# A list-scheduled attention and gated-graph kernel: the planner's figures for transfers, and the ranks of its last three batches

## The chip, the cores and the metric

The kernel runs on one core of a Trainium2 chip. Its time is the device time of one execution in microseconds, and of several executions the median is given. A core has a matmul engine (PE, with its weight loads as PEld), a vector engine (DVE), an activation engine (ACT), a general engine (POOL), and a queue engine (SP) that here only issues transfers. Each works through its own list of instructions in the order in which they were written. An instruction that waits for another engine or a transfer holds up everything behind it on its own engine.

## The reference

Two layers over 16 batches of 1024 nodes with 128 features, with one adjacency matrix of 1024 x 1024 for all:

```python
# layer 0: attention over pairs, then a residual and a layernorm
h = x @ others_weight
e = leaky_relu((h @ a1)[:, idx1] + (h @ a2)[:, idx2])
att = softmax(where(adj > 0, e, NEG_BIG), axis=1)
x = layernorm(x + att @ h + x @ self_weight)
# layer 1: five gated steps over the same graph, then a residual and a layernorm
def step(h):
    m_in = m_out = adj @ h
    av = concatenate([m_in, m_out], -1)
    u3 = h @ u3_w.T + u3_b
    z = sigmoid(av @ w3_w.T + w3_b + u3)
    r = sigmoid(av @ w4_w.T + w4_b + u3)
    hv = tanh(av @ w5_w.T + w5_b + (r * h @ u5_w.T + u5_b))
    return (1 - z) * h + z * hv
y = x
for _ in range(5):
    y = step(y)
x = layernorm(x + y)
```

Batches don't depend on each other. Within a batch the five steps do, each on the one before.

## The kernel before

Everything of a batch is kept as 128 partitions by 1024 columns and worked on in two halves of 512. The state is held twice: turned with features on the partitions (`hT`, 32-bit), and with nodes on the partitions as a pair of a rounded part and its remainder (`hN`), so that a product with the adjacency matrix can be made from two faster passes.

One step of one batch, `step(b, s)`: for each half, 16 matmuls of `hN` with the adjacency matrix (L888), copied to `m` by ACT (L906). Then, per half, a product of `hT` with the weights `u3` (L919), which ACT copies into a second accumulator (L922), so that the gate products of `m` (L929) are added onto it there; two tanh on ACT (L932) for r and z; r times `hT` on DVE (L939); two products into `ps_g_v` (L945 of `m`, L946 of r); a tanh on ACT (L949); three DVE operations (L956, L963, L970) that write the new `hT`. After that the state has to be turned into `hN` for the next step. `flip` does this in most places: DVE transposes blocks of 32 x 32 into `T` (L488), SP issues four stores of 64 KB into a buffer `D` in device memory in a permuted order (L493) and then one load of 256 KB back into `F` (L497), which waits for the stores. ACT casts `F` to the first part of `hN` (L507) and DVE subtracts for the second (L511); this is `split`. In the first two batches' layer 0, and in the last step of the last three batches, PE transposes instead (`on_pe`).

`layer0(b)` makes the attention layer: loads of `xt` (L526), a row vector brought to all partitions through device memory (`ud`, `pb`, `uu`: L583, L590, L597), the products at L759, and a layernorm whose statistics are on DVE (L451, L453), whose power is four POOL operations (L457 to L460), and whose scaling is on ACT (L465). The output layernorm works in the same way and ends in two stores on SP (L1013). Sixteen further loads of the adjacency matrix (`look`, L1033) feed a check of the input by DVE.

The order of all this isn't that of the loops. Every operation is given to `Plan.add` with an engine, a length in ns, a rank, what it reads and what it writes. `Plan.order` then plays the program through: whenever an engine is free it takes, of the operations that are ready, the one of lowest rank that finds its buffers free, and an operation becomes ready when the last that it depends on has ended, plus a lag. The order in which operations start there is the order in which they are written into the queues. Lags are per engine: from SP to anything 2500 ns, from PE 250, DVE 150, ACT 170, POOL 200. Lengths of DVE and ACT are taken times 1.2. So four stores of a flip count as 280 ns of SP and 2500 of lag, the load back as 70 and 2500, the load of `xt` as 2700 and 2500, and POOL's part of a layernorm as 2200 of POOL.

Ranks come from `rank_of(b, s)`, with a small addition for each kind of operation (0.3 for r, 0.8 for `split`, 4 for the output store, minus 7 for the first loads of layer 0). A batch starts 5 ranks after the one before, and a step 3 ranks after the one before, but for the last two batches. Buffers limit how many batches can be under way: four each of `hN`, `hT` and `y0`, three of `T` and `F`, six of `D`, six accumulators `ps`.

Of the kernel before, what the change touches and what calls it, by code (L numbers as in the profile page):

```python
# [30 lines left out]
class Plan:  # L31
# [11 lines left out]
    def __init__(self, slots):  # L43
        self.slots = dict(slots)
        self.ops = []
        self.writer, self.readers = {}, {}

    def add(self, engine, length, rank, emit, reads=(), writes=()):
        i = len(self.ops)
        deps = {self.writer[v] for v in reads if v in self.writer}  # L50
        for v in writes:
            deps |= self.readers.pop(v, set())
            if v in self.writer:
                deps.add(self.writer[v])
        for v in reads:
            self.readers.setdefault(v, set()).add(i)
        for v in writes:
            self.writer[v] = i
        deps.discard(i)
        tiles = {v[0] for v in (*reads, *writes) if v[0][0] in self.slots}  # L60
        if engine in ("DVE", "ACT"):
            length *= self.MARGIN
        self.ops.append((engine, length, rank, emit, deps, tiles))

    def order(self):
        ops, free = self.ops, dict(self.slots)
        users, left = [[] for _ in ops], []
        uses = {}
        for i, (_, _, _, _, deps, tiles) in enumerate(ops):
            left.append(len(deps))  # L70
            for d in deps:
                users[d].append(i)
            for t in tiles:
                uses[t] = uses.get(t, 0) + 1
        ready, busy, live = {}, {}, set()
        at = {}
        events = [(0, 0, i) for i in range(len(ops)) if not left[i]]
        heapq.heapify(events)
        started = []
        while events:  # L80
            now = events[0][0]
            while events and events[0][0] == now:
                _, what, i = heapq.heappop(events)
                engine, _, rank, _, _, tiles = ops[i]
                if what == 0:
                    heapq.heappush(ready.setdefault(engine, []), (rank, i))
                elif what == 1:
                    busy.pop(engine)
                    for t in tiles:
                        uses[t] -= 1  # L90
                        if not uses[t]:
                            free[t[0]] += 1
            more = True
            while more:
                more = False
                for engine, queue in ready.items():
                    if engine in busy:
                        continue
                    later = []
                    while queue:  # L100
                        rank, i = heapq.heappop(queue)
                        _, length, _, _, _, tiles = ops[i]
                        new = [t for t in tiles if t not in live]
                        if all(free[t[0]] > 0 for t in new):
                            for t in new:
                                free[t[0]] -= 1
                                live.add(t)
                            started.append(i)
                            busy[engine] = more = True
                            heapq.heappush(events, (now + length, 1, i))  # L110
                            for u in users[i]:
                                left[u] -= 1
                                lag = self.SAME[engine] if ops[u][0] == engine else self.LAG[engine]
                                at[u] = max(at.get(u, 0), now + length + lag)
                                if not left[u]:
                                    heapq.heappush(events, (at[u], 0, u))
                            break
                        later.append((rank, i))
                    for x in later:
                        heapq.heappush(queue, x)  # L120
        assert len(started) == len(ops)
        return started
# [3 lines left out]
def kernel(  # L126
# [52 lines left out]
    nc = tc.nc  # L179
    B = x_t.shape[0]  # L180
# [26 lines left out]
    def exact(pools):  # L207
# [45 lines left out]
        def T(t, dtype=None, shape=None):  # L253
            if t not in tiles:
                _, sh, dt, _ = kinds[t[0]]
                tiles[t] = places[t[0]].tile(
                    shape or sh, dtype or dt, tag=t[0], name="_".join(map(str, t)).replace("-", "n")
                )
            return tiles[t]
# [25 lines left out]
        def sp(*a, **k):  # L285
            plan.add("SP", *a, **k)
# [8 lines left out]

        def rank_of(b, s):

            if b >= B - 2:
                return 5 * B - 10 + 3.25 * s if b == B - 2 else 5 * B - 7 + 2.75 * s
            return 5 * b + 3 * s  # L300


        boot = ("hl", "boot")
# [14 lines left out]
        def early_loads():  # L318
# [28 lines left out]
            writes=[(boot, "early"), (ws, "early"), (x0, "early"), (("xt", 1), "early"), *((t, "early") for t in staged)],  # L347
# [134 lines left out]
        def flip(name, src, read, dst, write, rank):  # L482


            t, d = ("T", *name), ("D", *name)

            def turn():
                nc.vector.transpose(T(t).rearrange("p (b c i) -> p b c i", b=4, c=4), turned(src()))  # L488

            def away():  # L490
                swapped = T(d).rearrange("(b i) (a x) -> a i b x", b=4, a=4)
                for k in range(4):
                    nc.sync.dma_start(swapped[k], T(t)[32 * k : 32 * (k + 1), :].rearrange("i (b x) -> i b x", b=4))  # L493

            dve(V, rank, turn, reads=read, writes=[(t, 0)])
            sp(280, rank, away, reads=[(t, 0)], writes=[(d, 0)])
            sp(70, rank, lambda: nc.sync.dma_start(dst(), T(d)), reads=[(d, 0)], writes=[write])  # L497

        def split(b, s, g, src, read, rank):

# [16 lines left out]
        def layer0(b):  # L517

            first = rank_of(b, 0) - (60 if b == 0 else 0)
            rank = first + D["l1"]  # L520
            xt, hx, pb, u, us, uu, ud = (
                ("xt", b), ("hx", b), ("pb", b), ("u3", b), ("us", b), ("uu", b), ("ud", b)
            )
            q, zs, rz, yT, y0, hT = ("q", b), ("zs", b), ("rz", b), ("yT", b), ("y0", b), ("hT", b)
            if b >= 2:
                sp(2700, rank, lambda: nc.sync.dma_start(T(xt), x_t[b]), writes=[(xt, 0), (xt, 1)])  # L526

            for g in range(4):
                ph = ("ps", "g", b, "ph", g)
# [37 lines left out]
            if b >= 2:  # L567
# [10 lines left out]
                    280, rank, lambda: nc.vector.tensor_copy(T(us), T(put)[0 : 3 * NC, 0:P]), reads=[(put, 0)], writes=[(us, 0)]  # L578
                )
                sp(  # L580
                    60,
                    rank,
                    lambda: nc.sync.dma_start(T(ud).rearrange("t (c p) -> (t c) p", p=P), T(us)),  # L583
                    reads=[(us, 0)],
                    writes=[(ud, 0)],
                )
                sp(
                    60,
                    rank,
                    lambda: nc.sync.dma_start(T(pb), T(ud)[2:3, :].to_broadcast([P, N])),  # L590
                    reads=[(ud, 0)],
                    writes=[(pb, 0), (pb, 1)],
                )

                def uu_():
                    for w in range(2):
                        nc.sync.dma_start(T(uu)[:, w, :], T(ud)[w].rearrange("(c p two) -> two p c", p=P, two=2)[w])  # L597

                sp(120, rank, uu_, reads=[(ud, 0)], writes=[(uu, 0)])

            else:

# [275 lines left out]
        def step(b, s):  # L878
# [96 lines left out]
            for g in range(2):  # L975
                gs = slice(4 * g, 4 * g + 4)
                o = ("o", b)

                def h(g=g):
                    return T(hT)[:, g * HALF : (g + 1) * HALF]  # L980

                if on_pe(b, s):
                    t = ("ps", "t", b, s, g)
                    transposes(h, [(hT, g)], t, rank + D["tr"])

                    def n(t=t):
                        return T(t).rearrange("p (c a j) -> p c a j", c=4, a=4)

                else:
                    t = ("F", b, s, g)  # L990
                    flip((b, s, g), h, [(hT, g)], lambda t=t: T(t), (t, 0), rank + D["tr"])

                    def n(t=t):
                        return chunks(T(t))

                if s < STEPS - 1:
                    split(b, s + 1, g, n, [(t, 0)], rank + D["split"])
                    continue

                def last(n=n, g=g, gs=gs):  # L1000
                    dst = T(o)[:, gs, :].rearrange("p c (a j) -> p c a j", a=4)
                    nc.vector.tensor_tensor(dst, n(), T(y0)[:, gs, :].rearrange("p c (a j) -> p c a j", a=4), ALU.add)

                dve(V, rank + D["o"], last, reads=[(t, 0), (y0, g)], writes=[(o, "raw", g)])
                
                def at(j, g=g):
                    return T(o)[:, 4 * g + j, :]

                layernorm(o, g, rank + D["ln"], (o, "raw", g), at, at, (o, g))
                sp(  # L1010
                    60,
                    rank + D["out"],
                    lambda gs=gs: nc.sync.dma_start(  # L1013
                        out[b].rearrange("(c p) d -> p c d", p=P)[:, gs, :], T(o)[:, gs, :]
                    ),
                    reads=[(o, g)],
                )
# [332 lines left out]
```

## Time and profile before

| | |
|---|---|
| median of 3 runs | 1540.07 us (1539.38 to 1541.79) |
| the profiled execution | 1543.68 us, of which the span from the first to the last instruction is 1541.8 |
| mean granted clock of PE | 0.989 |
| PE, DVE, ACT, POOL busy | 1501.8, 991.0, 813.3, 150.3 us |
| matmuls | 5204 |
| longest waits of SP | for T from DVE 521.2 us, for stores into D to land 120.9, for the scaled output from ACT 114.4 |
| waits of ACT at the cast of hN for F | 221.5 us in 96 waits, the longest 9.0 |

Durations come from the one profiled execution, which was 3.6 us above the median. A matmul's recorded duration overlaps the next one's, so busy shares of PE near 100% say that it never stood still, and the time between two starts says what one costs. A line of the waits view reads: the engine and line that waited, for whom, us in total, number of waits, longest. In a timeline a row merges like instructions that follow each other.

### The profile page before, as it was taken

What the parts mean: (1) busy time and instruction counts of PE and PEld (TensorE: products, weight loads), DVE (VectorE), ACT (ScalarE), POOL (GpSimd) and SP (SyncE); (2) the same over time, 40 slices, a digit from 0 to 9 for tenths busy, and PEclk for the clock granted to TensorE, in tenths of its full rate; (3) what the DMA queues carried; (4) which work ended last, traced back from release to release, by engine and by line L of the source; (5) the groups of instructions that cost most, each with busy time, mean ns of one, the idle gap of its engine ahead of it and who ended that gap; (6) DMA issues with size and microseconds to landing.
All of it is one profiled execution on the core that took longest, in us unless ns stands there. A gap on an engine that the chain in (4) does not pass through costs nothing.

```text
span 1541.8 us, 17536 instructions
## 1 busy us (share of the span) xinstructions
PE 1501.8 (97%) x5204; PEld 947.1 (61%) x5204; DVE 991.0 (64%) x2438; ACT 813.3 (53%) x1656; POOL 150.3 (10%) x266
## 2 busy tenths in 40 slices
PE   9889999999999999999999999999999999999996
PEld 7556665666656666666566656656666566666563
DVE  6555777757566675756757566675756777554644
ACT  5554544556454555545555454555636565544544
POOL 0001010011110201111011110201111012000101
PEclk9889999999999999999999999999999999999998
DMA  4013444333433324334243433324334233322121
GB/s 170 26 50 100 115 134 139 92 107 90 110 96 93 100 75 116 95 91 113 74 116 89 114 92 89 102 74 119 90 92 114 69 105 109 96 80 65 47 76 36
DMA packets 193981, 144.83 MB, mean 94 GB/s; under 512 B 33279, under 2 KB 158934, under 8 KB 193878
## 3 DMA queue, kind: packets, MB, share of 16 engines
q1 hardware_dynamic: 193314, 142.78, 33.2%
q8 instruction: 43, 0.70, 0.2%
q10 hardware_dynamic: 564, 0.85, 0.2%
q14 instruction: 60, 0.49, 0.1%
HBM read 79.95 MB, written 63.61 MB: 93 GB/s over the span
## 4 chain that ended last, share of the span: by engine, by line
PE 60%; DMA 15%; DVE 10%; SPq 5%; ACT 4%; issue 3%; POOL 2%; ACTq 0%; DVEq 0%; POOLq 0%
PE ps_acc L888 24%; PE ps_acc_po L759 6%; PE ps_g_v L946 6%; PE ps_g_r L919 6%; PE ps_g_r L929 6%; PE gz L929 5%; PE ps_g_v L945 5%; DMA F<-D 5%; SPq L493 4%; DMA D<-T 3%; DMA uu<-ud 2%; DMA F_y<-D_y 1%; DVE hv L956 1%; DVE T L488 1%; DVE hv L963 1%
## 5 line engine op out<-in xcount | busy, mean ns | idle before, releaser
L888 PE MATMUL ps_acc<-adj,hN 128*128 128x512 f32 x2560 | 686.4, 420 | 0.7 <-ACT y L465 0.7
L888 PEld LDWEIGHTS ps_acc<-adj,hN 128*128 128x128 f32 x2560 | 483.7, 189 | 176.4 <-issue 65.1
L511 DVE TENSOR_TENSOR hN<-F,hN 128x512 fp32r<-128x512 f32 x128 | 88.5, 691 | 191.2 <-ACT hN L507 191.0
L507 ACT CAST hN<-F 128x512 fp32r<-128x512 f32 x128 | 79.1, 618 | 221.7 <-DMA F<-D 221.5
L906 ACT COPY m<-ps_acc 128x512 f32<-128x512 f32 x160 | 93.1, 583 | 177.8 <-PE ps_acc L888 177.8
L946 PE MATMUL ps_g_v<-r,u5h 128*128 128x512 f32 x320 | 164.6, 596 | 12.9 <-DVE r L939 12.9
L956 DVE TENSOR_TENSOR hv<-hv,hT 128x512 f32<-128x512 f32 x160 | 109.3, 683 | 104.8 <-ACT hv L949 104.6
L929 PE MATMUL ps_g_r<-m,wm 128*128 128x512 f32 x320 | 163.8, 593 | 0.8 <-ACT gz L922 0.7
L945 PE MATMUL ps_g_v<-m,wm 128*128 128x512 f32 x320 | 163.4, 592 | 0.0
L929 PE MATMUL gz<-m,wm 128*128 128x512 f32 x320 | 163.4, 592 | 0.0
L949 ACT ACTIVATE hv<-ps_g_v,b 128x512 f32<-128x512 f32 x160 | 109.0, 685 | 86.7 <-PE ps_g_v L946 86.1
L919 PE MATMUL ps_g_r<-hT,u 128*128 128x512 f32 x320 | 153.9, 601 | 0.7 <-ACT hT L871 0.7
L939 DVE SCALAR_TENSOR_TENSOR r<-r,hT 128x512 f32<-128x512 f32 x160 | 109.6, 687 | 58.1 <-ACT r L932 57.6
L759 PE MATMUL ps_acc_po<-adj,hl 128*128 128x512 f32 x512 | 138.5, 421 | 0.3 <-DVE hl L742 0.3
L932 ACT ACTIVATE r<-ps_g_r,bh 128x512 f32<-128x512 f32 x160 | 109.9, 689 | 29.0 <-PE ps_g_r L929 28.6
L759 PEld LDWEIGHTS ps_acc_po<-adj,hl 128*128 128x128 f32 x512 | 96.1, 188 | 36.3 <-issue 14.4
L946 PEld LDWEIGHTS ps_g_v<-r,u5h 128*128 128x128 f32 x320 | 59.9, 190 | 93.3 <-issue 58.1
L932 ACT ACTIVATE z<-gz,bh 128x512 f32<-128x512 f32 x160 | 108.8, 686 | 6.8 <-PE gz L929 6.8
L970 DVE SCALAR_TENSOR_TENSOR hT<-hv,hT 128x512 f32<-128x512 f32 x160 | 108.4, 678 | 5.3
L963 DVE SCALAR_TENSOR_TENSOR hv<-z,hv 128x512 f32<-128x512 f32 x160 | 107.9, 675 | 2.1
L488 DVE STREAM_TRANSPOSE T<-hT 128x512 f32<-128x512 f32 x154 | 108.4, 705 | 1.2
L929 PEld LDWEIGHTS gz<-m,wm 128*128 128x128 f32 x320 | 60.8, 190 | 76.5 <-issue 76.5
(134 smaller groups left out, 1309.9 us busy)
## 6 DMA issues: line engine op xcount, KB each, us to landing
D<-T SPq DMA_DIRECT2D x616, 64.0 KB
F<-D SPq DMA_DIRECT2D x154, 256.0 KB
out_dram<-o SPq DMA_DIRECT2D x32, 256.0 KB
xt<-in_x_dram SPq DMA_DIRECT2D x15, 512.0 KB
pb<-ud SPq DMA_DIRECT2D x14, 512.0 KB
D_y<-T_y SPq DMA_DIRECT2D x112, 64.0 KB
F_y<-D_y SPq DMA_DIRECT2D x28, 256.0 KB
D_b<-T_b SPq DMA_DIRECT2D x112, 64.0 KB
```

The costliest lines, as they stand in the source:

```text
L488: nc.vector.transpose(T(t).rearrange("p (b c i) -> p b c i", b=4, c=4), turned(src()))
L759: nc.tensor.matmul(T(po), hl[:, k, c, :], adj[:, c, hs], start=(first and i == 0), stop=(last and i == len(terms) - 1),)
L888: nc.tensor.matmul(T(pm), T(hN)[:, k, c, :], adj[:, c, hs[e]], start=(c == 0 and k == 0), stop=(c == NC - 1 and k == 1),)
L919: nc.tensor.matmul(T(pr), u3, h(), start=True, stop=True)
L929: nc.tensor.matmul(T(p_), wm[:, j, :], T(m), start=False, stop=True, skip_group_check=True)
L932: nc.scalar.activation(T(t), T(p_), AF.Tanh, bias=bh[:, j : j + 1], scale=0.5)
L939: lambda r=r, h=h: nc.vector.scalar_tensor_tensor(T(r), T(r), 1.0, h(), ALU.add, ALU.mult),
L945: nc.tensor.matmul(T(pv), wm[:, 2, :], T(m), start=True, stop=False)
L946: nc.tensor.matmul(T(pv), u5h, T(r), start=False, stop=True)
L949: nc.scalar.activation(T(hv), T(pv), AF.Tanh, bias=b5, scale=1.0)
L956: lambda hv=hv, h=h: nc.vector.tensor_tensor(T(hv), T(hv), h(), ALU.subtract),
L963: lambda hv=hv, z=z: nc.vector.scalar_tensor_tensor(T(hv), T(z), 1.0, T(hv), ALU.add, ALU.mult),
```

## The change

Three edits, none of which adds or removes an instruction. The planner can be told a lag for a single operation. The SP operations get other lengths and, some of them, such a lag. And the ranks of the last three batches are drawn from a start and an end for each, where the last two had their own formula.

```diff
-    def add(self, engine, length, rank, emit, reads=(), writes=()):
+    def add(self, engine, length, rank, emit, reads=(), writes=(), lag=None):
         i = len(self.ops)
+        if lag is not None:
+            self.lag[i] = lag
...
                                 lag = self.SAME[engine] if ops[u][0] == engine else self.LAG[engine]
+                                lag = self.lag.get(i, lag)
...
         def rank_of(b, s):
-            if b >= B - 2:
-                return 5 * B - 10 + 3.25 * s if b == B - 2 else 5 * B - 7 + 2.75 * s
-            return 5 * b + 3 * s
+            if b < B - 3:
+                return 5 * b + 3 * s
+            begin = 5 * b - 2 * (b - B + 3)
+            end = 5 * B + 4 - 2 * (B - 1 - b)
+            return begin + (end - begin) * s / 4
...
-            sp(280, rank, away, reads=[(t, 0)], writes=[(d, 0)])
-            sp(70, rank, lambda: nc.sync.dma_start(dst(), T(d)), reads=[(d, 0)], writes=[write])
+            sp(1830, rank, away, reads=[(t, 0)], writes=[(d, 0)], lag=1500)
+            sp(450, rank, lambda: nc.sync.dma_start(dst(), T(d)), reads=[(d, 0)], writes=[write], lag=2300)
...
-                sp(2700, rank, lambda: nc.sync.dma_start(T(xt), x_t[b]), writes=[(xt, 0), (xt, 1)])
+                sp(450, rank, lambda: nc.sync.dma_start(T(xt), x_t[b]), writes=[(xt, 0), (xt, 1)], lag=3500)
```

The store of `ud` goes from 60 to 450 ns, the load of `pb` from 60 to 450 with a lag of 3000, the two loads of `uu` from 120 to 950 with a lag of 3000, and the output store from 60 to 450. The loads of `look` keep 60 ns and 2500.

With B = 16 the ranks of steps 0 to 4 are:

| batch | before | after |
|---|---|---|
| 13 | 65, 68, 71, 74, 77 | 65, 68.75, 72.5, 76.25, 80 |
| 14 | 70, 73.25, 76.5, 79.75, 83 | 68, 71.5, 75, 78.5, 82 |
| 15 | 73, 75.75, 78.5, 81.25, 84 | 71, 74.25, 77.5, 80.75, 84 |

More of the change, by code (lines that the diff above doesn't have):

```diff
@@ L45, in __init__ @@
         self.ops = []
+        self.lag = {}
         self.writer, self.readers = {}, {}
-    def add(self, engine, length, rank, emit, reads=(), writes=()):
+    def add(self, engine, length, rank, emit, reads=(), writes=(), lag=None):
         i = len(self.ops)
+        if lag is not None:
+            self.lag[i] = lag
         deps = {self.writer[v] for v in reads if v in self.writer}
@@ L580, in layer0 @@
                 sp(
-                    60,
+                    450,
                     rank,
@@ L587, in layer0 @@
                 sp(
-                    60,
+                    450,
                     rank,
@@ L592, in layer0 @@
                     writes=[(pb, 0), (pb, 1)],
+                    lag=3000,
                 )
@@ L597, in uu_ @@
                         nc.sync.dma_start(T(uu)[:, w, :], T(ud)[w].rearrange("(c p two) -> two p c", p=P, two=2)[w])
-                sp(120, rank, uu_, reads=[(ud, 0)], writes=[(uu, 0)])
+                sp(950, rank, uu_, reads=[(ud, 0)], writes=[(uu, 0)], lag=3000)
             else:
@@ L1010, in step @@
                 sp(
-                    60,
+                    450,
                     rank + D["out"],
```

## The prediction

> **What bounds the kernel now.** I read the page's busy shares first, then the busy time by stretch, then the waits of the matmul engine, then the timeline around one such wait, and last the timeline of the end.
>
> ```profile
> PE 1501.8 (97%) x5204; PEld 947.1 (61%) x5204; DVE 991.0 (64%) x2438; ACT 813.3 (53%) x1656; POOL 150.3 (10%) x266
> ```
>
> The matmul engine is the bound: no edit removes a matmul, so all that can be won is time in which it stands still or runs at half clock. Where that time lies is in the busy time by stretch (length, then busy time of each engine, then the granted clock):
>
> ```profile
> 50.00:100.00 50.00, 44.71 (x157) 30.92 (x156) 26.84 (x79) 22.93 (x53) 3.76 (x8) 0.87 0.16 43
> ...
> 200.00:250.00 50.00, 47.52 (x163) 29.60 (x162) 37.32 (x90) 23.13 (x45) 6.33 (x8) 0.97 0.52 152
> ...
> 1000.00:1200.00 200.00, 195.68 (x668) 122.34 (x666) 130.68 (x320) 108.21 (x223) 21.20 (x37) 1.00 0.37 100
> ...
> 1400.00:1500.00 100.00, 100.00 (x326) 60.36 (x325) 53.97 (x94) 47.99 (x81) 3.93 (x8) 1.00 0.22 62
> ...
> 1526.50:1541.80 15.30, 1.31 (x8) 0.84 (x8) 6.60 (x23) 3.79 (x9) 3.41 (x8) 0.63 0.16 47
> ```
>
> Length less PE: 5.3 us in 50 to 100; 2.5 in 200 to 250; in the four stretches from 250 to 1000, 1.4, 1.3, 2.6 and 1.5; 4.3 in 1000 to 1200; 0.1 in 1200 to 1300; nothing from 1300 to 1500. So 13.7 us between 200 and 1300, none in the last three batches, and 14.0 us of drain after the last gate matmul. The waits of PE name the middle part:
>
> ```profile
> PE ps_g_v L946 <- DVE r L939: 12.9, 11, 2.4
> PE ps_g_ph L534 <- ACT y L465: 4.6, 1, 4.6
> ```
>
> Asked window by window, the eleven are 2.4 (at 240 us), then once per batch 1.4, 0.8, 0.5, 0.7, 1.5, 0.7, 0.8, 1.2, 1.0, 1.8. The last, in the timeline (start, duration, engine; idle time ahead in brackets):
>
> ```profile
> 1186.77 1.66 ACT L465 ACTIVATE o<-o,rstd_o 128x128 f32<-128x128 f32 x4 [2.96 <-POOL rstd_o L460]
> ...
> 1188.45 2.84 SPq L1013 DMA_DIRECT2D out_dram<-o  x2
> ...
> 1189.66 0.70 DVE L488 STREAM_TRANSPOSE T<-hT 128x512 f32<-128x512 f32 x1
> ...
> 1191.39 1.92 SPq L493 DMA_DIRECT2D D<-T  x4
> ...
> 1194.79 0.34 SPq L497 DMA_DIRECT2D F<-D  x1
> ...
> 1197.48 0.62 ACT L507 CAST hN<-F 128x512 fp32r<-128x512 f32 x1 [4.75 <-DMA F<-D]
> 1198.01 0.58 ACT L906 COPY m<-ps_acc 128x512 f32<-128x512 f32 x1
> 1198.14 0.69 DVE L511 TENSOR_TENSOR hN<-F,hN 128x512 fp32r<-128x512 f32 x1 [2.65 <-ACT hN L507]
> 1198.49 0.69 ACT L932 ACTIVATE r<-ps_g_r,bh 128x512 f32<-128x512 f32 x1
> ...
> 1200.10 1.13 PE L946 MATMUL ps_g_v<-r,u5h 128*128 128x512 f32 x2 [1.83 <-DVE r L939]
> ```
>
> To be seen: ACT stands 4.75 us at the cast of hN, whose reload has not landed, while the gate r behind it is long ready. The written order puts the cast first because the planner expected the reload earlier. The transpose is done at 1190.36 and the reload lands at 1197.46: 7.10 us, of which 1.03 is SP standing behind the two output stores. The planner reckons 150 + 280 + 2500 + 70 + 2500 = 5500 ns for it.
>
> **What the Trainium skill says.** "Perfetto Trace Analysis", section Sequencer Loop: an engine's instruction waits in its queue for its semaphores; the trace agrees (the cast holds up m and r). "DMA: Bandwidth & Descriptors", Anatomy of one DMA, puts about 2.0 us of fixed cost on a transfer, mostly the write's receipt; here the last store's issue to the reload's issue is 1.48 us and the reload's issue to the cast 2.35 us, so the new lags (1500, 2300) are what this trace shows. "TensorE: Matmul & The Clock Gate", What's actually happening, has the clock halved after an idle window of about 3.4 us; here a wait of 2.35 us at 242.8 already halved it for four matmuls (L919 x4 takes 3.57 us against 1.88 elsewhere: 1.7 us), and 1.83 us at 1200 didn't. The measurement decides.
>
> **The change part by part.** No instruction is added or removed; only the order in the queues moves. The words name gate sums in PSUM, but no line of the diff touches them: the gate matmuls at L929 already add onto a copied sum. That part is nothing.
>
> 1. Flips. Planned time of one becomes 150 + 1830 + 1500 + 450 + 2300 = 6230 ns, 0.73 more. Casts move behind what is ready up to 0.73 us sooner, so each per-batch wait shrinks by 0.73 or vanishes: seven times 0.73, and 0.5, 0.7, 0.7, together 7.0 us. A vanished wait also saves its restart (1197.67 to 1200.10 is 2.43 us between starts against 0.43 unhindered, 2.0 lost for 1.83 shown, and 0.1 on the next): 0.3 each, three times, 0.9. Two waits of L929 on gz (0.3 each, 0.2 of restart) go: 1.0. Taken: 8.9. Bounds: 0 (the rest of the lateness, ACT and POOL, is as before) and 18 (all 13.7 with fourteen restarts at 0.3).
>
> 2. SP's order. Planned now at 1.83 us for four stores, SP no longer takes a flip's stores in 0.28. The two halves' transposes end 3.07 us apart (1190.36, 1193.43), and the first reload becomes ready 1.83 + 1.5 = 3.33 after its stores began: the second half's stores go ahead of the first reload. First half about 1.6 us later, second about 0.6 earlier; the product needs both, so I count nothing, bounds minus 0.6 and plus 1.6 per step where PE has no other batch's work. Between 250 and 1200 it has some: PE is 99% busy. Behind a store that waits stand all loads, xt, pb and uu too.
>
> 3. xt: 5.2 us planned becomes 3.95, and no longer blocks SP for 2.7. In 50 to 100 us, PE waits 4.6 us for ps_g_ph, then runs at clock 0.87 in that stretch. That chain (product, transposes, statistics, POOL, scale) has no transfer, but the reload of batch 0 that PE needs next is issued at 78.90 behind xt. I take 2 us won, between 0 and 6. Loads pb and uu move with lags of 3.0 for 2.5: nothing, hidden under the one rank between load and use, some 18 us (five ranks, a batch, take about 92 us in the trace); look loads keep 60 and 2500, and the 240 us wait (2.4 + 0.3 + 1.7) starts at one: nothing, bounds minus 4.4 and plus 4.4.
>
> 4. Ranks of the last three. Batch 13 slows, 14 and 15 start two ranks earlier; matmuls are the same. PE has no idle there to win. What must keep covering: from the end of batch 15's step 3 gates to its last product.
>
> ```profile
> 1493.64 8.02 PE L888 MATMUL ps_acc<-adj,hN 128*128 128x512 f32 x32
> ...
> 1505.75 0.69 DVE L511 TENSOR_TENSOR hN<-F,hN 128x512 fp32r<-128x512 f32 x1 [0.38 <-ACT hN L507]
> ...
> 1509.68 0.80 PE L888 MATMUL ps_acc<-adj,hN 128*128 128x512 f32 x1
> ```
>
> Batch 14's last step fills the 16.0 us between; the operand is ready after 12.8, so 3.2 spare. In the new ranks 82 still lies between 80.75 and 84, so the cover stays: nothing. If it went, 12.8 us would lie bare. A gain is excluded but for 0.5, since the drain is the same chain.
>
> Sum: 8.9 + 2 = 10.9 us less. Against the profiled execution, 1543.68, that is 1532.8; the median of the runs is 3.6 lower, so 1529.
>
> **The rivals.**
> A (forecast): part of the waits goes. 1529, own range 1522 to 1536.
> B: all waits of the middle (18 + 1.7 of clock) and the 6 us near the start go: 1540 - 25.7 = 1514. For: the new lags are the measured ones. Against: the cast above was late by over 3 us (the product that m reads ended at about 1193.97: start 1189.68 and 4.29), not 0.73, and POOL's part is still planned at 2200 ns where it took 3.0 (1183.71 to 1186.73).
> C: waits wander to other places, size kept: 1539. For: each order is one throw of a greedy list; against: ten waits have one cause, and the edit aims at it.
> D (slower): the output stores. Flips planned longer on SP sort more often behind both output stores of a finished batch, which wait for the scale on ACT and so for POOL; reloads then land later than planned and r waits behind the cast. From a PE wait of about 2.35 us on, the clock halves too: a batch goes from 1.05 us to 2.35 + 1.7, plus 3.0. At five of ten batches 15 us, 1555. Place: after each batch's last step. For: 1.03 us of it is there now; against: the new plan knows of 1.8 us more SP time per flip.
>
> **How the numbers follow.** Chances: A 0.50, B 0.12, C 0.17, D 0.21. About 0.2% (3.1 us) is what a measurement of this kernel can tell from no change. A is faster but for 0.01 same; B faster; C 0.05 faster, 0.08 same, 0.04 slower; D slower. Together 0.66, 0.09, 0.25. Low end 1513, for B; high end 1545, which leaves out most of D (0.17) and a little of B (0.03).
>
> **What would show it.** Right: PE's waits on L939 fall from 12.9 to about 6 us, the idle of ACT ahead of the cast of hN falls from 221.5 us by some 70 (0.73 for each of 96 waits), and 1300 to 1526 stays full. Wrong: waits of over 2.3 us with a clock below 1.00 in some stretch after 100 us; idle PE in the last 60 us (step 4); second-half stores not ahead of first reloads (step 2); or PE busy shares by stretch that don't move.

## The result, and the profile after

| | before | after |
|---|---|---|
| median of 4 runs | 1539.72 us | 1522.21 us (1520.58 to 1525.58) |
| profiled execution, and its span | 1543.68, 1541.8 us | 1525.58, 1523.8 us |
| matmuls | 5204 | 5204 |

The ratio of after to before is 0.9896, with a 95% interval of 0.9863 to 0.9929: faster by about 1%, or 17.5 us. It lies at the lower edge of the forecast's own range (1522 to 1536); the forecast was 1529.

The same two views of the changed kernel, first the page's busy shares, then the busy time by stretch (length; busy time of PE, PEld, DVE, ACT, POOL; granted clock):

```profile
PE 1496.8 (98%) x5204; PEld 947.5 (62%) x5204; DVE 988.6 (65%) x2438; ACT 824.4 (54%) x1656; POOL 146.3 (10%) x266
```

```profile
50.00:100.00 50.00, 44.18 (x154) 30.45 (x153) 26.46 (x79) 22.77 (x53) 3.40 (x8) 0.86 0.16 43
...
200.00:250.00 50.00, 49.98 (x176) 31.34 (x175) 39.22 (x95) 26.03 (x49) 4.37 (x8) 1.00 0.53 155
...
1000.00:1200.00 200.00, 200.00 (x701) 127.64 (x700) 137.69 (x353) 114.22 (x242) 21.79 (x40) 1.00 0.36 100
...
1400.00:1500.00 100.00, 100.00 (x335) 61.39 (x334) 53.69 (x100) 47.31 (x80) 3.92 (x8) 1.00 0.21 58
```

The reader is to see that the middle is full. From 200 to 1300 us the matmul engine stood still for 13.7 us before and for 0.02 us after, and the clock in 200 to 250 is 1.00 instead of 0.97. That is 13.7 of the 18.0 us by which the span shrank. From 200 us to the end of the last gate matmul it took 1326.3 us before and 1308.6 after, so nearly all was won there; what goes beyond the 13.7 fits restarts after waits and the matmuls at half clock, which busy time doesn't show, but it was not itemised. The start is no better in this profile (44.18 us busy in 50 to 100, 44.71 before), nor is the drain: from the end of the last gate matmul to the end of the span it is 15.2 us, 15.5 before.

The waits view of the changed kernel has no line any more of PE waiting for the gate r (L939 before, now L946). What is left is the start:

```profile
PE ps_g_ph L540 <- ACT y L471: 5.5, 2, 4.3
```

and ACT, which stood 221.5 us ahead of casts, stands there for a fifth of it, and waits for PE instead (177.8 us before):

```profile
ACT m L913 <- PE ps_acc L895: 249.9, 113, 6.3
...
ACT hN L513 <- DMA F<-D: 45.3, 44, 4.0
```

The timeline of the changed kernel at the place that answers to the wait shown before, where a finished batch is normalised and stored while another batch turns its state:

```profile
1174.34 1.65 ACT L471 ACTIVATE o<-o,rstd_o 128x128 f32<-128x128 f32 x4
...
1176.00 0.70 DVE L494 STREAM_TRANSPOSE T<-hT 128x512 f32<-128x512 f32 x1
1176.02 0.39 SPq L1020 DMA_DIRECT2D out_dram<-o  x1
...
1176.73 1.79 SPq L499 DMA_DIRECT2D D<-T  x4
...
1178.56 0.45 SPq L1020 DMA_DIRECT2D out_dram<-o  x1
...
1179.12 1.93 SPq L499 DMA_DIRECT2D D<-T  x4
...
1181.17 0.38 SPq L503 DMA_DIRECT2D F<-D  x1
```

```profile
1184.57 0.63 ACT L513 CAST hN<-F 128x512 fp32r<-128x512 f32 x1
1185.09 0.95 ACT L550 COPY hx<-ps_g_ph 128x262 f32<-128x262 f32 x3
1186.51 0.69 ACT L939 ACTIVATE r<-ps_g_r,bh 128x512 f32<-128x512 f32 x1 [0.48 <-PE ps_g_r L936]
```

Two things are different. The flip's four stores are issued between the two output stores, 0.03 us after their transpose ended (1176.70), where they stood 1.03 us behind both of them before. And the cast finds its reload landed: no idle time in brackets. The next r waits for PE, not the other way round. In the order of SP's transfers, a flip's stores stand between a batch's two output stores in 1 of 16 batches before and in 12 of 16 after.

### The profile page after: what moved, and what is told of

The parts are those of the page before. It is cut to its first block, busy times and chain, and to the rows that moved or that the text cites. A ratio compares the mean times of both kernels' runs of the same rounds, so it can differ in the third digit from the quotient of the medians.

```text
span 1523.8 us, 17516 instructions
## 1 busy us (share of the span) xinstructions
PE 1496.8 (98%) x5204; PEld 947.5 (62%) x5204; DVE 988.6 (65%) x2438; ACT 824.4 (54%) x1656; POOL 146.3 (10%) x266
## 4 chain that ended last, share of the span: by engine, by line
PE 95%; DMA 2%; DVE 1%; POOL 1%; ACT 0%; SPq 0%; issue 0%; POOLq 0%
PE ps_acc L895 39%; PE gz L936 9%; PE ps_g_r L936 9%; PE ps_g_r L926 9%; PE ps_g_v L953 9%; PE ps_g_v L952 9%; PE ps_acc_po L766 7%; PE ps_g_ph L540 1%; PE ps_acc_px L808 1%; PE ps_acc_po L822 1%; DMA hN_boot<-in_adj_dram 1%; DMA hl_boot<-in_L_gnn_w_w_dram 1%; DMA D<-T 0%; DVE junk L695 0%; ACT y L471 0%
## 5 line engine op out<-in xcount | busy, mean ns | idle before, releaser
L946 DVE SCALAR_TENSOR_TENSOR r<-r,hT 128x512 f32<-128x512 f32 x160 | 109.3, 685 | 116.4 <-ACT r L939 115.9
L939 ACT ACTIVATE r<-ps_g_r,bh 128x512 f32<-128x512 f32 x160 | 110.1, 688 | 39.9 <-PE ps_g_r L936 39.5
L939 ACT ACTIVATE z<-gz,bh 128x512 f32<-128x512 f32 x160 | 107.6, 686 | 11.7 <-PE gz L936 11.3
L929 ACT COPY gz<-ps_g_r 128x512 f32<-128x512 f32 x160 | 90.8, 571 | 35.7 <-PE ps_g_r L926 34.7
```

The lines of the kernel that those rows point to most:

```text
L939: nc.scalar.activation(T(t), T(p_), AF.Tanh, bias=bh[:, j : j + 1], scale=0.5)
L946: lambda r=r, h=h: nc.vector.scalar_tensor_tensor(T(r), T(r), 1.0, h(), ALU.add, ALU.mult),
```

## The experiments

All start from the kernel before and leave the rest of it as it was, but for the second and the last, which start from the changed one. The theory: casts of `hN` are written ahead of work that is ready, because the planner lands their reloads too early. The rivals: the ranks; the other transfers; SP's time as against the landing; and that any new order would have done. The runs were made in three groups, each with runs of the kernel before beside it (medians 1540.15, 1542.04 and 1541.31 us); the ratios refer to these. Across groups a difference of 1 or 2 us between two medians says little.

| run | median, us | range | ratio to before, 95% interval |
|---|---|---|---|
| ranks only | 1543.29 | 1539.02 to 1547.55 | 1.0006 to 1.0027 |
| all but the ranks | 1524.34 | 1523.91 to 1525.79 | 0.9871 to 0.9922 |
| flip only | 1522.20 | 1521.05 to 1522.53 | 0.9852 to 0.9903 |
| flip, by lags only | 1521.22 | 1520.38 to 1523.37 | 0.9846 to 0.9898 |
| flip, SP's time only | 1522.78 | 1522.24 to 1525.70 | 0.9848 to 0.9892 |
| flip shorter | 1608.02 | 1604.48 to 1612.93 | 1.0394 to 1.0462 |
| flip halfway | 1521.23 | 1520.60 to 1523.18 | 0.9841 to 0.9887 |
| flip longer | 1527.08 | 1524.01 to 1527.68 | 0.9869 to 0.9918 |
| POOL 3000 | 1519.60 | 1517.47 to 1521.34 | 0.9810 to 0.9894 |
| last step's flips | 1530.81 | 1526.29 to 1533.33 | 0.9904 to 0.9950 |
| other steps' flips | 1528.76 | 1527.95 to 1529.22 | 0.9892 to 0.9940 |
| flip and ranks | 1519.31 | 1518.86 to 1519.38 | 0.9813 to 0.9895 |

### Which edit carries it

**Ranks only.** The diff is that of `rank_of` alone.

> The new ranks of the last three batches on the planner's old figures for transfers. Theory (the gain comes from casts that the planner no longer places ahead of their reloads): 1538 to 1542 us, PE still waits about 13 us for L939, once per batch. Rival (the ranks carry a good part of the 17.5 us): 1533 us or less, with less idle PE already before 1200 us.

Measured: 1543.29 us, slower by 0.16% with an interval clear of 1. PE's waits for r stay (11.1 us in 10 waits), and 14.3 us are idle from 200 to 1300. The order of the matmuls is that of the kernel before until 1139 us. The ranks don't carry the gain.

**All but the ranks.**

```diff
-            if b < B - 3:
-                return 5 * b + 3 * s
-            begin = 5 * b - 2 * (b - B + 3)
...
+            if b >= B - 2:
+                return 5 * B - 10 + 3.25 * s if b == B - 2 else 5 * B - 7 + 2.75 * s
+            return 5 * b + 3 * s
```

> All new figures for SP's transfers, old ranks. Theory: 1521 to 1524 us, like the changed kernel, PE's waits between 200 and 1200 us gone. Rival of the ranks: 1530 us or more. If the old end suffers under the longer planned transfers (two batches only, so PE planned idle), idle PE between 1300 us and the end, some 5 to 12 us, so 1527 to 1534.

Measured: 1524.34 us, about 2 us above the changed kernel, a difference that these two runs can't separate (their ranges overlap). From 1300 to 1500 PE stands idle for 1.0 us, where it had none.

**Flip only.**

```diff
-            sp(280, rank, away, reads=[(t, 0)], writes=[(d, 0)])
-            sp(70, rank, lambda: nc.sync.dma_start(dst(), T(d)), reads=[(d, 0)], writes=[write])
+            sp(1830, rank, away, reads=[(t, 0)], writes=[(d, 0)], lag=1500)
+            sp(450, rank, lambda: nc.sync.dma_start(dst(), T(d)), reads=[(d, 0)], writes=[write], lag=2300)
```

> Only the flip's two figures are new (stores 1830 and lag 1500, reload 450 and lag 2300); xt, ud, pb, uu, the output store and the ranks as before. Theory: 1521 to 1526 us, waits of PE for L939 below 2 us. Rival (the loads of xt, pb and uu, or the output store, planned truly, do it): 1533 to 1540 us, waits of 8 us or more stay.

Measured: 1522.20 us, the whole gain. The planned figures of the other transfers aren't needed. Whether they would have won something without the flip's was not tried.

### What in the flip's figures counts

**By lags only**: lengths stay 280 and 70, and the lags become 3050 and 2680.

> Flip planned with the new time from transposed to reloaded (6080 ns on SP and in flight), but with the old lengths on SP (280 and 70), the rest of it put into the lags (3050 and 2680); all else as before. If the later landing is what counts: 1521 to 1528 us, waits for L939 below 3 us. If it is SP's time that the planner now sees (stores of several flips and outputs can't all go at once): 1533 to 1540 us, waits of 8 us or more.

Measured: 1521.22 us. The later landing is enough without SP's time.

**SP's time only**: lengths 1830 and 450, lags 950 and 2120, so that a lone flip lands at 5350 ns as before.

> Flip's stores and reload planned with the new lengths on SP (1830 and 450), but with lags cut to 950 and 2120, so that a lone flip is planned to land at 5350 ns as before. Theory (the planned landing decides): 1532 to 1540 us, with waits for L939 of 4 us or more left; a part may go because the second flip of a pair is now planned behind the first on SP. Rival (any truer or just other order does it): 1521 to 1526 us.

Measured: 1522.78 us, the whole gain again, which the theory in that form did not expect. With 1830 ns on SP, flips that meet are planned to land one after another, so some land later even though a lone one doesn't; that this is how it works here was not shown. What its trace shows is the new order of most of the faster runs: a flip's stores between the output stores in 10 of 16 batches.

**Shorter**: lengths 280 and 70, lags 2135 and 2135, so 4620 ns.

> Flip planned 0.73 us shorter than before (280 + 2135 + 70 + 2135 = 4620 ns), all else as before. Theory: casts stand still earlier in the order, each of the ten waits grows by up to 0.73 us and more waits appear: 1547 to 1565 us, with half clock where a wait passes 2.3 us. Rival (each order is one throw, the old one was an unlucky one): as likely 1520 to 1530 us.

Measured: 1608.02 us, 66 us slower, more than expected. The waits view and a long stretch of the middle:

```profile
PE ps_g_v L950 <- DVE r L943: 45.6, 23, 3.4
```

```profile
200.00:1300.00 1100.00, 1048.54 (x3526) 650.05 (x3524) 697.18 (x1703) 573.42 (x1140) 107.61 (x182) 0.98 0.34 95
```

51.5 us are idle where 13.7 were, in waits of up to 3.4 us, and the clock of the whole stretch falls to 0.98: after some of these waits the matmuls run at half clock for a while. Flips stand between the output stores in 2 of 16 batches. But the longest waits, of 2.6 to 3.4 us, don't lie behind the output stores. One of them, with no output store issued between 1050 and 1130 us:

```profile
1111.49 0.62 ACT L511 CAST hN<-F 128x512 fp32r<-128x512 f32 x1 [4.03 <-DMA F<-D]
...
1116.15 0.62 ACT L511 CAST hN<-F 128x512 fp32r<-128x512 f32 x1 [1.77 <-DMA F<-D]
1116.67 0.58 ACT L910 COPY m<-ps_acc 128x512 f32<-128x512 f32 x1
...
1117.15 0.69 ACT L936 ACTIVATE r<-ps_g_r,bh 128x512 f32<-128x512 f32 x1
...
1118.62 1.13 PE L950 MATMUL ps_g_v<-r,u5h 128*128 128x512 f32 x2 [3.14 <-DVE r L943]
...
1119.59 1.02 PE L949 MATMUL ps_g_v<-m,wm 128*128 128x512 f32 x2
```

Here casts placed too early hold up r without any output store. Planning a flip 0.73 us shorter costs three to four times what planning it 0.73 us longer won.

**Halfway**: lags 2865 and 2500, so 5715 ns.

> Flip planned halfway (280 + 2865 + 70 + 2500 = 5715 ns), all else as before. Theory as worked in the prediction, each wait shorter by the planned difference: 1534 us, waits of 6 to 9 us left. If a small shift lets the cast change places with m and r behind it, and the whole wait goes at once: 1521 to 1526 us.

Measured: 1521.23 us, again the whole gain. One wait of 1.7 us for r is left from 200 to 1300, and no other idle time. So the waits don't shrink in proportion to the shift: those that came once per batch leave at once.

**Longer**: lags 3550 and 3180, so 7080 ns.

> Flip planned one us longer than in the change (280 + 3550 + 70 + 3180 = 7080 ns, the time that the reload of the wait shown in the profile before took), all else as before. Theory: no cast stands in the way, 1520 to 1526 us, ACT's idle before the cast below 100 us. If planning too late costs (states reach the product later, PE without work near the start or the end): 1527 to 1535 us, idle PE before 100 us or after 1300.

Measured: 1527.08 us, the second of the two outcomes. Casts cost ACT only 37.0 us of idle time there, but PE is idle for 2.0 us from 200 to 1300 (none with the lags at 6080 ns) and 4.0 us in 50 to 100 (2.8 there). Between 5715 and 6080 ns the time is flat; at 7080 it is about 6 us worse, of which these two explain only a part. The order on SP is nearly the old one, with a flip's stores between the output stores in 1 of 16 batches. What is new is the cast: in the ten batches that waited for r before, the first cast behind the output stores now finds its reload landed.

### Which part of the cycle makes the wait

**POOL 3000.** No transfer figure is touched.

```diff
-            plan.add("POOL", 2200, rank, power, reads=[(mv, 0)], writes=[(rstd, 0)])
+            plan.add("POOL", 3000, rank, power, reads=[(mv, 0)], writes=[(rstd, 0)])
```

> The kernel before, with only POOL's part of a layernorm planned at 3000 ns instead of 2200; no transfer figure is touched. If the casts are what is planned too early: 1536 to 1543 us, waits for L939 of 8 us or more. If any shift of the order by under a microsecond ends the per-batch wait, or if it was POOL's lateness that made it: 1520 to 1528 us.

Measured: 1519.60 us. This is the run that changes the theory. ACT still stands 193.6 us ahead of casts, nearly as long as before (221.5), yet the middle is full but for 2.0 us. Its timeline at the same place:

```profile
1167.44 0.38 SPq L1013 DMA_DIRECT2D out_dram<-o  x1
...
1167.86 1.98 SPq L493 DMA_DIRECT2D D<-T  x4
...
1169.95 0.40 SPq L1013 DMA_DIRECT2D out_dram<-o  x1
...
1174.66 0.62 ACT L507 CAST hN<-F 128x512 fp32r<-128x512 f32 x1 [2.93 <-DMA F<-D]
...
1175.66 0.69 ACT L932 ACTIVATE r<-ps_g_r,bh 128x512 f32<-128x512 f32 x1
```

```profile
1176.46 1.02 PE L945 MATMUL ps_g_v<-m,wm 128*128 128x512 f32 x2
1177.32 1.08 PE L946 MATMUL ps_g_v<-r,u5h 128*128 128x512 f32 x2
```

The cast is still ahead of m and r and still waits, but for 2.93 us instead of 4.75, and r comes in time: L946 follows L945 without a wait in brackets. What moved is SP. Planned later, the second output store has fallen behind the flip's stores, so these no longer stand behind a store that waits for ACT, and ACT for POOL. It is so in 11 of 16 batches. Not all of the gain lies in the middle, however: the order is new from 40 us on, and in the first 200 us 768 matmuls are started (744 before). Priced at the median time between starts of each kind of matmul, that is by my estimate about 7 of the 22 us by which the span shrank.

**Last step's flips**: lags 3050 and 2680 where `name[1] == STEPS - 1`, the default elsewhere.

> The later landing (lags 3050 and 2680) for the flips of a batch's last step alone, whose reload feeds the output sum on DVE (L1002) and not a cast; steps 0 to 3 and layer 0 as before. If the wait starts with that sum standing on DVE for its reload (3.55 us in the wait shown), and the late cast only follows: 1521 to 1528 us. If it is the casts: 1536 to 1543 us.

Measured: 1530.81 us, about half of the gain and neither of the two outcomes. A flip's stores stand between the output stores in 11 of 16 batches, and the wait for r once per batch is gone; one wait of 2.7 us for r, four of 2.0 together for gz, and the start as before are left. In all 4.3 us are idle from 200 to 1300. The matmuls stand in exactly the order of the kernel before, so what this run won came from the order on SP, ACT and DVE alone.

**Other steps' flips**: the same lags where `name[1] in range(STEPS - 1)`.

> The counterpart: the later landing for the flips of steps 0 to 3 alone, whose reloads feed the casts. If it is the casts: 1520 to 1526 us, waits for L939 below 3 us. If the last step's sum starts the wait: 1532 to 1542 us.

Measured: 1528.76 us. The middle is full but for 0.6 us, and this without a flip's stores between the output stores in any batch; here the cast was placed later and stands 2.29 us (it starts at 1183.17) at the place where it stood 4.75. The loss is nearer the start:

```profile
100.00:200.00 100.00, 95.39 (x313) 58.95 (x312) 73.74 (x178) 49.34 (x99) 6.08 (x8) 0.98 0.41 116
```

4.6 us idle and a clock of 0.98 in a stretch in which the kernel before had none.

**Flip and ranks**: the flip's figures and the new `rank_of`, without the figures for xt, ud, pb, uu and the output store.

> The flip's new figures and the new ranks, without the new figures for xt, ud, pb, uu and the output store. The flips alone left 46.6 us of busy PE in 50 to 100 us (44.2 in the changed kernel) and 0.9 us idle after 1300 with the old ranks (0.0 in the changed kernel). If both add up: 1519 to 1521 us, below either. If each order makes its own small losses: 1521 to 1526 us.

Measured: 1519.31 us. Its stretches, and below them those of the flip alone:

```profile
50.00:100.00 50.00, 47.18 (x176) 32.66 (x175) 31.60 (x98) 25.81 (x63) 3.57 (x8) 0.93 0.22 64
...
1300.00:1500.00 200.00, 200.00 (x656) 121.64 (x655) 103.25 (x194) 97.47 (x167) 12.63 (x24) 1.00 0.22 62
```

```profile
1300.00:1500.00 200.00, 199.08 (x652) 120.60 (x651) 104.81 (x199) 95.04 (x160) 9.79 (x22) 1.00 0.23 64
```

PE is busy 3.0 us more in 50 to 100 than in the changed kernel (44.18), and the 0.9 us idle after 1300 are gone. Its four runs lie below all runs of the flip alone and of the changed kernel. But its matmuls stand in the same order as those of the flip alone until 1118 us, and by there its profiled run is already 1.6 us ahead, which the ranks can't have done. This run and POOL 3000 have the lowest medians, 2 to 3 us below the change. That either is faster than the change is not shown: they were run at different times, the intervals of the ratios overlap, and POOL 3000's runs overlap with those of the change.

### What this says together

Once per batch, a chain runs through four engines: the last step's reload, the sum on DVE, POOL, the scale on ACT, the output stores on SP, and behind these the stores of another batch's flip, its reload, its cast, and r behind the cast. The planner was early at several links. In the order before, the wait reached PE where two things came together: the flip behind both output stores, and the cast ahead of r by too much. The kernel before shows it by itself: its first batch, the only one with a flip's stores between the output stores, has no wait for r behind them, and each of the ten after it has one. (The last five have none either; there the casts behind the output stores wait 0.9 us at most.) The changed kernel and the runs that won most show the first undone, with a flip between in 10 to 13 of 16 batches; the other steps' flips and the longer flip (0 and 1 of 16) show the second. The shorter flip shows that a cast far enough ahead of r makes PE wait without the first. Since the order repeats from batch to batch, undoing it once undoes it in nearly every batch. One thing stays open. Every run that altered the middle altered a planned time in this chain; none altered it by something unrelated. So it isn't excluded that the old order was in part an unlucky one. It can't have been chance alone: planned shorter it lost 66 us, and none of the runs that planned part of this chain longer lost.

## Why the prediction was right or wrong

**The bound, and where the time lay.** Right: the middle gave what was won, the last three batches had nothing to give, and the drain stayed.

**Step 1, the flips.** Right in the cause, wrong in the size, and this is the term that failed: 8.9 us taken, with a bound of 18, where 17.7 were won from 200 us to the last gate matmul. The step took 0.73 us off each wait, as if a cast that is planned later arrived later by the same amount. A list order has no such slope. The halfway run shows it: with half the shift, the waits once per batch were gone whole. The 17.7 us are 13.7 of idle time, 1.7 of half clock, and so at most some 2.3 of restarts, where the bound had 4.2. The two waits on gz went as forecast. The rival B had this size for the middle but put 6 us of the start on top.

**Step 2, SP's order.** The forecast that the second half's stores would pass the first half's reload came true at the place shown (stores at 1176.73 and 1179.12, then the reload at 1181.17; before, a reload stood between them), but not everywhere: at 1101 us in the changed kernel it is stores, reload at 1104.26, stores at 1104.93, and at the start the reload goes first too. It was counted at nothing, and no run priced it alone. What mattered on SP was the order against the output stores. The prediction saw 1.03 us there and used it for the slower rival D, which did not come. The later plan moved the flips ahead of the second output store, not behind it.

**Step 3, xt and the start.** 2 us taken, nothing clear came: 44.18 us busy in 50 to 100 after 44.71. All but the ranks, whose matmuls stand in the order of the changed kernel until 1121 us, has 45.72 there, so one order varies by 1.5 us in this stretch. Added to the flip's figures, those of the other transfers cost about 2 us (1524.34 with them against 1522.20 without, run in the same group, ranges apart). So for this group of transfers the sign was wrong; which of them it was, and whether xt, was not tried. The look wait at 240 us, counted at nothing, went: 2.5 us idle in 200 to 250 before, none after.

**Step 4, the ranks.** Taken at nothing. Alone they cost 0.16%. With the flip's figures they win a little near the end, where longer planned flips leave the old two-batch end about 1 us idle. Up to the 3901st matmul old and new ranks give one order of the matmuls. From there to the end of the span the new ones take 1.6 us less beside the flip's figures alone (402.15 after 403.73), 1.8 less beside all figures, and 2.6 more beside none, by one profile each. The step had excluded a gain of more than 0.5. The cover of 16 us held.

**The rivals.** C, waits that wander, is out: the middle is empty of them. Half clock after waits, D's price, came in the run with the shorter flip, on the other side of the old figure. But no length of about 2.35 us divides the waits. In that run 1.84 us brought it (two matmuls take 1.91 us next, 1.02 elsewhere), while the wait of 3.14 us shown above did not (1.02 next):

```profile
1311.52 1.69 PE L933 MATMUL ps_g_r<-m,wm 128*128 128x512 f32 x2 [1.84 <-ACT gz L926]
1313.00 1.91 PE L933 MATMUL gz<-m,wm 128*128 128x512 f32 x2
```

**The signs named beforehand.** PE's waits for r fell to nothing, not to 6 us; ACT's idle time ahead of casts fell by 176 us, not 70. That second sign was a poor one: the flip alone leaves 111.7 us of it and POOL 3000 193.6, both with a middle full to within 2 us.

**The number.** 10.9 us were forecast and 17.5 came. The direction was right, and so were the place of the main gain and its cause. That the number still fell within the range, at its edge, was partly luck: the main term was half of what came, and the 2 us of step 3, which did not come, covered some of what it lacked.

## What to carry to other kernels

In this kernel's planned order, a duration planned too short was far dearer than one too long: against the figure that the kernel had, 0.73 us less cost 66 us, 0.4 to 0.7 more won about 20 (ratios of 0.986 and 0.987), and 1.7 more won 16 (0.989). Look for a wait that returns once per iteration and follow it over all engines to the in-order queue where something ready stands behind something that waits; one link planned truly can clear it everywhere. Don't take the shift in a planned time as the gain: bound it by the whole wait.

## What the runs showed of the hardware that was not expected

The same four POOL steps of a layernorm half took 1.94 us at the end of the kernel before (1531.67 to 1533.61), and 3.02 us in the middle (1183.71 to 1186.73), where DVE was busy with two-input operations: single steps of 0.23 became 0.50, of 0.24 became 0.65. That is more than the 0.73 us which the flips' figures were changed by, and planning for it alone won as much in all as planning the transfers truly. In the whole profile before there are 256 such steps. With next to no two-input operation beside them (117 steps) each took its short time of 0.23, 1.04, 0.24 or 0.20 us, also in the 30 cases in which DVE was busy with other operations. Those that ran for more than 70% beside two-input operations took 0.54, 1.46, 0.59 and 0.49 us in the mean.
